# Four fused attention layers on one core: layer 3's mask tables tied to their row of layer 2, and the values of layer 3's first two rows made in layer 2's last row

## The chip, the core and the metric

The kernel runs on one core of a Trainium2 chip. The metric is device time in microseconds of one execution. A core has five engines that run their own instruction streams in order and meet through semaphores: PE (TensorE, matrix products), DVE (VectorE), ACT (ScalarE), POOL (GpSimd) and SP (SyncE, which here only issues transfers between memory and the core's SBUF). PE writes its products to PSUM, from which DVE and ACT read them.

## The reference

Four images of 56 x 56 pixels with 256 channels go through four layers, each of the form x = x + f(group norm of x). Layer 2 is neighbourhood attention (a 7 x 7 window around every pixel, half of the heads dilated by 2), layer 3 is attention in shifted 7 x 7 windows with a position bias and a mask. What the change touches, cut from the reference:

```python
# layer 3, on the group norm of layer 2's result
xs = jnp.roll(x, (-3, -3), axis=(1, 2))              # then cut in windows of 7 x 7
qkv = xw @ qkv_weight.T + qkv_bias
q, k, v = (qkv[0] * hd ** (-0.5), qkv[1], qkv[2])
attn = jnp.einsum('whnd,whmd->whnm', q, k) + bias    # bias = rel_bias_table[rel_index]
attn = attn.reshape(B, nW, HEADS, N, N) + mask[None, :, None]
attn = jax.nn.softmax(attn, axis=-1)
out = jnp.einsum('whnm,whmd->wnhd', attn, v)
out = out @ proj_weight.T + proj_bias                # rolled back, and x = x + out
...
x = x + _L2_conv_ref(_gn(x), ...)
x = x + _L3_conv_ref(_gn(x), ...)
```

## The kernel before, in words

`direct_blocks` runs the layers one after the other, with all activations in float32 and the images handed from layer to layer through DRAM.

**Layer 2** (`layer2`) goes through 16 rows (4 images, 4 strips of 14 image rows). In this text row r is one of the 16, and unit r.u is one of its 8 units of attention, u = 0 to 7. `attend_pairs` takes the units in turn. For unit u it issues the logits (PE, L1067, into `ps_s`, of which there is one pair); DVE adds a bias to one half of them (L1074) and ACT takes the exponential (L1075); of the other half ACT takes the exponential first (L1077) and POOL multiplies it (L1078). Then POOL adds up pairs of the unit before (`both`, L1087), the unit's extra work is issued (`fill`), and PE makes the products of the unit before (L1096). After them come DVE's reciprocal (L1960), ACT's look at it (L998) and DVE's scaling into `attn` (L1964, L1970). The gathers of a unit's values from DRAM (`vp<-vd`, L1954, SP) go to one of three buffers, so a gather can be issued when the products of the third unit before are done.

The extra work of a row is laid out in `work[0]` to `work[7]`: projecting the input of a row ahead (`project_rows`: values L979, keys and queries L952), normalising one more (`prepare`, ACT, L942), and the output projection of the row before (`project_out`, L952 and then DVE L1995 and L896, in four steps at u = 2, 3, 6, 7). Rows 14 and 15 have nothing left to project: row 14 has `project_rows` work in its first half only, row 15 only output projections. After the last row come the tail (`both` and `products` of unit 15.7) and the output projection of row 15.

In rows 1 to 4, `work[7]` also takes a step of `table_steps`: layer 3's mask tables. Each of four steps adds a table to the looked up bias on DVE (L2058, two instructions), takes an exponential of part of it on ACT (L2060) and stores it to `m3d` in DRAM (L2062). The order of layer 2 on each engine comes from a scheduler that works with its own estimates of time and puts an instruction where it finds it ready. It put all four steps right at the start of layer 2, and likewise layer 3's load of the first half of the tables (`m3a`, L2097).

**Layer 3** (`layer3`) goes through 32 rows of 7 image rows, in an order that is written out by hand for PE, DVE, ACT and POOL. Before its first attention it has a head: `prepare(0)` and `prepare(1)` normalise two rows on DVE (L945, six instructions each), `values` of rows 0 and 1 (PE L979, DVE L983, stored to DRAM L987, read back in another layout by `gather`, L2147), the keys and queries of row 0 (`project_rows(0)`), and `prepare(2)`.

SBUF is handed out in pools that are closed in the reverse order of opening. Layer 2's input pool (`brief`: `xn2`, `v2`, `q2`) stands on the left side and stays open until layer 2 ends; layer 3's pools stand on the right.

Of the kernel before, what the change touches and what calls it, by code (L numbers as in the profile page):

```python
# [830 lines left out]
def direct_blocks(ctx: ExitStack, tc: tile.TileContext, d: dict, watch):  # L831
# [136 lines left out]

    def value_tiles(v, a, c, n, xn, w, bias, dst):

        t0, t1 = c * n // P, (c + 1) * n // P if (c + 1) * n < T else -(-T // P)
        pm = ps_m()
        sizes = [min(P, T - t * P) for t in range(t0, t1)]
        mine = sizes[2 * a:2 * a + 2]
        for j, k in enumerate(mine):
            first = (2 * a + j) * P
            for h in range(CC):
                for i in range(0, k, HD):
                    nc.tensor.matmul(pm[i:i + HD, j * C:(j + 1) * C], lhsT=xn[:, h, first + i:first + i + HD], rhs=w[:, h, :],  # L979
                                     start=(h == 0), stop=(h == CC - 1))  # L980
        for k in sorted(set(mine)):
            js = [j for j, kj in enumerate(mine) if kj == k]
            nc.vector.tensor_tensor(  # L983
                v[:k, 2 * a + js[0]:2 * a + js[-1] + 1, :], pm[:k, js[0] * C:(js[-1] + 1) * C].rearrange("p (j c) -> p j c", c=C),
                bias[:k].rearrange("p (o c) -> p o c", o=1).to_broadcast([k, len(js), C]), ALU.add)
            t = t0 + 2 * a + js[0]
            nc.sync.dma_start(out=dst[t * P:min((t + len(js)) * P, T), :].rearrange("(k p) c -> p k c", p=k),  # L987
                              in_=v[:k, 2 * a + js[0]:2 * a + js[-1] + 1, :])
# [64 lines left out]

    def attend_pairs(pool, units):

# [47 lines left out]
        for w in units:  # L1103
# [7 lines left out]
            held = w  # L1111
        both(held)
        products(held)
        held["done"]()
# [736 lines left out]

    def layer2(held, big, pool, brief, last_steps, ends):

        nonlocal m_bufs
        m_bufs = 2
        xs, load, w_qkv, bias = (held[n] for n in ("xs", "load", "w", "bias"))
        xns, q, attns, ahead = {}, {}, {}, []
# [127 lines left out]
        def project_out(r):  # L1985
# [13 lines left out]
            return [lambda m=m, y=y: step(y, m) for y in range(2) for m in range(CC)]  # L1999

        def stream():
            n = NIMG * NSB
            for r in range(n):
                attns[r] = pool.tile([P, CC, 2 * WC2], FP, tag="attn", name="attn2")
                work = [[] for _ in range(8)]
                for y, i in enumerate((2 * r + 3, 2 * r + 4)):
                    if i < 2 * n:
                        v0, v1, k0, k1, q0, q1 = lazily(project_rows, i, 6)
                        for a, steps in enumerate(((v0, k0), (v1, q0), (k1,), (q1,))):
                            work[4 * y + a] += steps  # L2010
                    if i + 1 < 2 * n:
                        work[4 * y + 3].append(lambda i=i: prepare(i + 1))
                if r:
                    for u, step in zip((2, 3, 6, 7), project_out(r - 1)):
                        work[u].append(step)
                for u in (1, 4, 5):
                    work[u].insert(0, step_stats)
                if r and table:
                    work[7].append(table.pop(0))
                for u, w in enumerate(pair(r, m, i) for i in range(4) for m in range(2)):  # L2020
                    w["fill"] = lambda steps=work[u]: [f() for f in steps]
                    yield w
# [15 lines left out]
        table.append(tables.close)  # L2038
        attend_pairs(pool, stream())
        for step in project_out(NIMG * NSB - 1):  # L2040
# [5 lines left out]
    def table_steps(big, pool):  # L2046
# [7 lines left out]
        def mask(ty):  # L2054
            m = pool.tile([98, NH, 98], FP, tag="m3", name="m3")
            for w in range(2):
                sl = slice(w * WN, (w + 1) * WN)
                nc.vector.tensor_tensor(m[:, :, sl], found.rearrange("p q h -> p h q"), t3[:, ty:ty + 1, sl].to_broadcast([98, NH, WN]), ALU.add)  # L2058
            mv = m.rearrange("p (q j) k -> p q j k", j=4)[:, :, 2:4]
            nc.scalar.activation(mv, mv, AF.Exp)  # L2060
            for pair in [3] if ty % 2 else range(3):
                nc.sync.dma_start(out=m3d[:, ty // 2, :, pair, :], in_=m)  # L2062
# [13 lines left out]

    def layer3(early, big, pool, brief):
        def image_rows(wr):
# [8 lines left out]

        xs, xns, vs, qk, attns, ahead = {}, {}, {}, {}, {}, []
        vd = [dram.tile([T, C], FP, name=f"vd3_{b}") for b in range(NIMG)]
# [4 lines left out]

        load(0)
        m3 = [big.tile([98, NH, 4 * 98], FP, name="m3a")]
        nc.sync.dma_start(out=m3[0], in_=m3d[:, 0].rearrange("p h w k -> p h (w k)"))  # L2097
        w_qkv = weight(early, "wqkv3", 3 * C)
        w_p = weight(pool, "wp3", C)
        m3.append(pool.tile([98, NH, 4 * 98], FP, name="m3b", bufs=1))  # L2100
        nc.sync.dma_start(out=m3[1], in_=m3d[:, 1].rearrange("p h w k -> p h (w k)"))

# [7 lines left out]

        def prepare(r):
            x = xs.pop(r)
            if r + 1 < NIMG * 8:
                load(r + 1)
            c = r % 8
            xn = xns[r] = early.tile([P, CC, 448], FP, tag="xn", name="xn3", bufs=3)
            at = left(c, WC)
            for h in range(CC):
                for w, xv in parts(xn[:, h, at:at + WC], x[:, h, :]):
                    normalise(w, xv, known(3, r // 8), h)  # L2120
            if at:
                end = left(c - 1, WC) + WC
                nc.scalar.copy(xn[:, :, :at], ahead[0][:, :, end - at:end])
            ahead[:] = [xn]

        def project_rows(r):
# [22 lines left out]
        def values(r):  # L2149
# [5 lines left out]
            def step(a):  # L2155
                value_tiles(v, a, c, WC, xn, w_qkv[:, :, 2 * C:], bv3, vd[b])
                if a == 0 and r:
                    gather(r - 1)
# [4 lines left out]
        def quad(r, hq, single=False):  # L2163
# [22 lines left out]

            mk = m3[wr // 7][:, 4 * hq:4 * hq + 4, :]
            i = 2 * (NIMG * 8 + r) + hq
# [56 lines left out]

        prepare(0)
        prepare(1)
        for r in range(2):
            for step in values(r):
                step()  # L2250
        for step in project_rows(0):
# [26 lines left out]

    ends, firsts, passing, begun = ExitStack(), ExitStack(), ExitStack(), []

    def begin_layer1():
# [5 lines left out]
        begun[:] = [[few] + first, late]  # L2287
        return steps

    def run(l, layer, fixed, kinds):  # L2290
# [16 lines left out]
    with pool_of(2, 0) as early:  # L2307
        held = {}
        last_steps = run(1, lambda own: layer1(*own, first, late, lambda: layer2_ahead(early, held)), {E.PE, E.DVE}, range(3))
        firsts.close()  # L2310
        run(2, lambda own: layer2(held, *own, last_steps, ends), None, range(1, 4))
    run(3, lambda own: layer3(own[1], own[0], *own[2:]), {E.PE, E.DVE, E.Activation, E.Pool}, (1, 0, 2, 3))
    return newest[0].ins
# [101 lines left out]
```

## Time and profile before

| what | us |
|---|---|
| median of 3 runs | 3770.52 (3767.21 to 3772.34) |
| the profiled execution | 3769.93 |
| its span | 3768.0 |
| PE busy | 3665.8 (97%) |
| DVE busy | 2200.9 (58%) |
| ACT busy | 1472.2 (39%) |
| POOL busy | 1815.9 (48%) |

Layer 2 begins in the span at about 2600 us and layer 3's head at about 3250 us. Two stretches around these points, and one of layer 2's steady part between them:

| stretch, us | PE busy | DVE | ACT | POOL | granted PE clock |
|---|---|---|---|---|---|
| 2628 to 2670 (42.0) | 35.21 | 24.40 | 24.28 | 25.19 | 0.96 |
| 2670 to 2710 (40.0) | 39.95 | 28.41 | 27.89 | 32.61 | 1.00 |
| 3215.4 to 3245.4 (30.0), row 15 | 26.55 | 24.73 | 15.91 | 29.17 | 0.94 |
| 3245.4 to 3257.6 (12.2), tail and output projection | 10.58 | 9.33 | 2.08 | 3.58 | 0.72 |

A row of this kind gives the busy time of each engine in the stretch, and the share of its full clock that PE was granted. A timeline row gives start and length of an instruction, or of several of one kind that follow each other (x4), the engine ("SPq" is SP issuing a transfer, "PEld" PE loading weights), the line, what is written from what, and in brackets the idle time before it with what ended it. The profile counts a float32 matmul as two passes.

### The profile page before, as it was taken

Reading aid. Unit: us, or ns where it says so; the run is one execution under the profiler, and the core shown is the slowest. Engines: PE = TensorE matmul, PEld = TensorE weight load, DVE = VectorE, ACT = ScalarE, POOL = GpSimd, SP = SyncE. Lnnn points to the kernel's source line nnn. Section 1 sums busy time; section 2 is a strip of 40 time slices with the busy share of each in tenths; the row PEclk is TensorE's granted clock in tenths of the full one; section 3 lists DMA queues with packets and bytes.
Section 4 is the critical chain, followed back from the end, with each engine's and each line's share of the span. In section 5 each row is a group of like instructions: output and inputs, shape, how many; then the busy total and the mean of one; then the engine's idle time right before and its main releaser. Section 6 shows DMA issues by size and latency. Waiting matters only on the chain. (4 is left out here: it accounts for less than half of the span.)

```text
span 3768.0 us, 112324 instructions
## 1 busy us (share of the span) xinstructions
PE 3665.8 (97%) x48826; PEld 2478.1 (66%) x48826; DVE 2200.9 (58%) x4188; ACT 1472.2 (39%) x3125; POOL 1815.9 (48%) x1966
## 2 busy tenths in 40 slices
PE   8999999999999999999999999999999999999998
PEld 4555556677776777767777667775666666555554
DVE  5777777634445444464344544445676777777676
ACT  5565566422222222222222222222666666444443
POOL 4777777612235222352222421123777777555555
PEclk9999999999999999999999999999999999999999
DMA  6544444300010000011000000002544444534443
GB/s 213 169 153 134 132 123 137 134 7 23 23 27 29 22 19 18 21 32 28 19 16 22 26 20 10 11 20 78 138 133 137 132 128 119 155 126 139 130 134 99
DMA packets 278039, 304.94 MB, mean 81 GB/s; under 512 B 33624, under 2 KB 268764, under 8 KB 277084
## 3 DMA queue, kind: packets, MB, share of 16 engines
q1 hardware_dynamic: 275680, 297.43, 25.7%
q8 instruction: 385, 6.31, 0.7%
q0 software_dynamic: 1568, 0.16, 0.1%
q14 instruction: 118, 0.97, 0.1%
q10 hardware_dynamic: 288, 0.08, 0.0%
HBM read 205.04 MB, written 92.55 MB: 79 GB/s over the span
## 5 line engine op out<-in xcount | busy, mean ns | idle before, releaser
L1564 DVE TENSOR_TENSOR acc<-acc,ps_v 128x257 f32<-128x257 f32 x1104 | 463.8, 422 | 781.8 <-PE ps_v L1642 753.4
L1642 PE MATMUL ps_v<-xw,e 128*128 128x257 f32 x2208 | 611.0, 381 | 3.4 <-DVE xnT L1509 2.2
L1637 PE MATMUL ps_o<-xw,at 128*128 128x257 f32 x2208 | 609.0, 379 | 0.0
L1532 PE MATMUL ps_s<-xnT,xd 128*128 128x512 f32 (+3 forms) x1344 | 571.4, 548 | 3.9 <-DVE xnT L1509 3.9
L1626 ACT COPY at<-ps_t 128x512 f32<-128x512 f32 (+3 forms) x332 | 170.6, 514 | 960.9 <-PE ps_t L1623 960.7
L1642 PEld LDWEIGHTS ps_v<-xw,e 128*128 128x128 f32 x2208 | 413.4, 189 | 144.6 <-issue 83.2
L1087 POOL TENSOR_TENSOR b<-e 126x336 f32<-126x336 f32 (+5 forms) x512 | 499.5, 997 | 7.7
L1637 PEld LDWEIGHTS ps_o<-xw,at 128*128 128x128 f32 x2208 | 419.1, 190 | 60.1
L952 PE MATMUL ps_m<-xn,w_wqkv 128*32 128x392 f32 x4096 | 376.4, 496 | 8.0 <-ACT gst L917 3.4
L1525 POOL TENSOR_SCALAR xd<-xnT,vec 128x128 f32<-128x128 f32 x192 | 116.4, 616 | 478.0 <-PE ps_s L1532 477.8
L1078 POOL TENSOR_TENSOR e<-e,m0t 126x672 f32<-126x672 f32 (+3 forms) x128 | 238.8, 1865 | 182.1 <-ACT e L1077 180.6
L1535 ACT ACTIVATE e<-ps_s 128x512 f32<-128x512 f32 x336 | 185.4, 552 | 355.0 <-PE ps_s L1532 351.8
L1532 PEld LDWEIGHTS ps_s<-xnT,xd 128*128 128x128 f32 x1344 | 225.4, 191 | 141.4 <-issue 126.2
L1078 POOL TENSOR_TENSOR e<-e,bias 119x784 f32<-119x784 f32 (+5 forms) x128 | 239.4, 1870 | 157.3 <-ACT e L1077 156.9
L1096 PEld LDWEIGHTS ps_o<-e,vp 124*32 124x32 f32 (+3 forms) x8192 | 200.3, 110 | 101.9 <-issue 84.1
L998 ACT ACTIVATE no<-rs 128x168 f32<-128x168 f32 (+2 forms) x256 | 94.0, 367 | 426.0 <-DVE rs L1960 190.2
L952 PEld LDWEIGHTS ps_m<-xn,w_wqkv 128*32 128x32 f32 x4096 | 123.8, 110 | 183.1 <-issue 128.6
L1960 DVE RECIPROCAL rs<-ps_o 128x196 f32<-128x196 f32 (+2 forms) x128 | 175.7, 1372 | 109.7 <-PE ps_o L1096 108.0
L1096 PE MATMUL ps_o<-e,vp 124*32 124x112 f32 (+3 forms) x8192 | 232.2, 249 | 3.1 <-POOL e L1078 2.5
L1075 ACT ACTIVATE e<-e 126x672 f32<-126x672 f32 (+5 forms) x256 | 219.7, 858 | 13.3 <-DVE e L1074 1.9
L1077 ACT ACTIVATE e<-ps_s 126x672 f32<-126x672 f32 (+5 forms) x256 | 206.3, 806 | 5.4 <-PE ps_s L1067 3.0
L979 PE MATMUL ps_m<-w_wqkv,xn 128*32 128x256 f32 x3136 | 196.9, 381 | 2.1 <-DVE v L983 1.6
(214 smaller groups left out, 5945.5 us busy)
## 6 DMA issues: line engine op xcount, KB each, us to landing
x<-xr SPq DMA_DIRECT2D x64, 392.0 KB
x<-in_x SPq DMA_DIRECT2D x53, 448.0 KB
x<-x SPq DMA_DIRECT2D x60, 392.0 KB
xr<-x SPq DMA_DIRECT2D x60, 392.0 KB
vd<-v SPq DMA_DIRECT2D x72, 256.0 KB
xr<-in_x SPq DMA_DIRECT2D x32, 392.0 KB
xr<-x SPq DMA_DIRECT2D x28, 448.0 KB
x<-xr SPq DMA_DIRECT2D x28, 448.0 KB
```

What stands on the lines that cost most here:

```text
L952: nc.tensor.matmul(pm[j * HD:(j + 1) * HD, :n], lhsT=w[:, h, col + j * HD:col + (j + 1) * HD], rhs=rhs(h), start=(h == 0), stop=(h == CC - 1))
L979: nc.tensor.matmul(pm[i:i + HD, j * C:(j + 1) * C], lhsT=xn[:, h, first + i:first + i + HD], rhs=w[:, h, :], start=(h == 0), stop=(h == CC ...
L1075: nc.scalar.activation(ev, ev, AF.Exp)
L1077: nc.scalar.activation(ev, sv, AF.Exp)
L1078: nc.gpsimd.tensor_tensor(parts(ev), parts(ev), w["emask"], ALU.mult)
L1087: nc.gpsimd.tensor_tensor(w["b"][a][:nk, :, :2 * nq].rearrange("p h (i c) -> p h i c", i=2), ev[:, :, :, 0, :], ev[:, :, :, 1, :], ALU.add)
L1096: nc.tensor.matmul(w["o"](k, i)[j * HD:(j + 1) * HD], lhsT=ones[:nk, :HD] if k else v(j, u), rhs=w["b"][j // 2][:nk, j % 2, i * nq:(i + 1) ...
L1532: nc.tensor.matmul(s[:, :n], lhsT=xd[j][:, h, :], rhs=xnT[:, h, first * P:last * P], start=(h == 0), stop=(h == CC - 1))
L1535: nc.scalar.activation(e[:, :n], s[:, :n], AF.Exp, scale=5.0)
L1564: nc.vector.tensor_tensor(acc[:, i, :], acc[:, i, :], pv[:, :C + 1], ALU.add)
L1637: nc.tensor.matmul(out[j][:, :C + 1], lhsT=e[:, col(i)] if i == j else at[:, col(i)], rhs=xw[:, i, :], start=(i == j), stop=(i == NB - 1))
L1642: nc.tensor.matmul(pv[:, :C + 1], lhsT=e[:, col(i)], rhs=xw[:, j, :], start=True, stop=True)
```

## The change

1. The two additions of a mask step get an edge behind the newest bias addition of layer 2 on DVE (`tc.issue_after(newest[0].ins)`), so that each step stands in its own row, 1 to 4.
2. Layer 2 opens its input pool itself (`passing`) and closes it in unit 14.4, when the last input is projected. The queries of rows 14 and 15 move to a small pool on the right (`d2q`). The first part of layer 3 (`layer3_ahead`) opens its pools there, over the closed pool's memory.
3. In units 14.4 to 14.7 the first steps of layer 3 are issued: the loads of its first rows, its qkv weights in three parts, `prepare(0)` and `prepare(1)`, now on ACT, and the load of half of the first mask table (`m3a` is split in `m3a` and `m3c`, four heads each).
4. The values of layer 3's rows 0 and 1 are made in six steps of one or two tiles: at u = 0, 1, 4, 5 of row 15 and two in the tail, between `both` and `products`. Layer 3's head keeps `gather(0)`, `project_rows(0)` and `prepare(2)`.
5. In row 14 the four steps of the output projection stand at u = 4, 5, 6, 7 instead of 2, 3, 6, 7.

```diff
-    def value_tiles(v, a, c, n, xn, w, bias, dst):
+    def value_tiles(v, a, c, n, xn, w, bias, dst, some=range(2), pm=None):
-        pm = ps_m()
+        pm = ps_m() if pm is None else pm
...
         for j, k in enumerate(mine):
+            if j not in some:
+                continue
...
+        if len(mine) - 1 not in some:
+            return pm
...
-    def attend_pairs(pool, units):
+    def attend_pairs(pool, units, tail=()):
...
         both(held)
+        for step in tail:
+            step()
         products(held)
...
-    def layer2(held, big, pool, brief, last_steps, ends):
+    def layer2(held, big, pool, last_steps, ends, begin_layer3):
+        passing, values3 = ExitStack(), []
+        brief = passing.enter_context(pool_of(2, 3))
...
+        def begin():
+            passing.close()
+            steps3[:], values = begin_layer3(1)
+            values3.extend(values)
+            steps3[0]()
...
+                if r == n - 4:
+                    q[n - 2], q[n - 1] = begin_layer3(0)
...
-                    for u, step in zip((2, 3, 6, 7), project_out(r - 1)):
+                    for u, step in zip((4, 5, 6, 7) if r == n - 2 else (2, 3, 6, 7), project_out(r - 1)):
                         work[u].append(step)
+                if r == n - 2:
+                    work[4].append(begin)
+                    for u in range(1, 4):
+                        work[4 + u].append(lambda u=u: steps3[u]())
+                if r == n - 1:
+                    for u in (0, 1, 4, 5):
+                        work[u].append(lambda: values3.pop(0)())
...
-        attend_pairs(pool, stream())
+        attend_pairs(pool, stream(), [lambda: values3.pop(0)()] * 2)
...
-                nc.vector.tensor_tensor(m[:, :, sl], found.rearrange("p q h -> p h q"), t3[:, ty:ty + 1, sl].to_broadcast([98, NH, WN]), ALU.add)
+                with tc.issue_after(newest[0].ins):
+                    nc.vector.tensor_tensor(m[:, :, sl], found.rearrange("p q h -> p h q"), t3[:, ty:ty + 1, sl].to_broadcast([98, NH, WN]), ALU.add)
...
-        m3 = [big.tile([98, NH, 4 * 98], FP, name="m3a")]
-        nc.sync.dma_start(out=m3[0], in_=m3d[:, 0].rearrange("p h w k -> p h (w k)"))
-        w_qkv = weight(early, "wqkv3", 3 * C)
+        m3 = big.tile([98, 4, 4 * 98], FP, name="m3a")
+        w_qkv = early.tile([P, CC, 3 * C], FP, name="w_wqkv3", bufs=1)
+        def load_weight(k):
...
-        def prepare(r):
+        def prepare(r, normal=normalise):
...
-                    normalise(w, xv, known(3, r // 8), h)
+                    normal(w, xv, known(3, r // 8), h)
...
+        def values(r):
+            v, pms = own.tile([P, 4, C], FP, tag="vt", name="vt3", bufs=1), []
+            def step(a, some, *pm):
+                pms.append(value_tiles(v, a, r, WC, xns[r], w_qkv[:, :, 2 * C:], bv3, vd[0], some, *pm))
+            return [lambda: step(0, (0,)), lambda: step(0, (1,), pms[0]), lambda: step(1, (0,))]
+
+        steps = [lambda: (load(0), load_weight(2)), lambda: (prepare(0, normalise_act), load_weight(1)),
+                 lambda: (prepare(1, normalise_act), load_weight(0)),
+                 lambda: nc.sync.dma_start(out=m3, in_=m3d[:, 0, :4].rearrange("p h w k -> p h (w k)"))]
+        return [transfer, xns, vd, m3, w_qkv, parts, prepare], steps, lazily(values, 0, 3) + lazily(values, 1, 3)
+
+    def layer3(front, pool):
+        m3 = [[m3, pool.tile([98, 4, 4 * 98], FP, name="m3c", bufs=1)]]
+        nc.sync.dma_start(out=m3[0][1], in_=m3d[:, 0, 4:].rearrange("p h w k -> p h (w k)"))
...
-        prepare(0)
-        prepare(1)
-        for r in range(2):
-            for step in values(r):
-                step()
+        gather(0)
         for step in project_rows(0):
             step()
         prepare(2)
...
+    def begin_layer3(part):
+        open_pool = lambda name, bufs: fronts.enter_context(
+            tc.tile_pool(name=name, bufs=bufs, side="right", reuse_waits="tile"))
+        if part == 0:
+            few = open_pool("d2q", 1)
+            return [few.tile([P, CC, 2 * WC2], FP, name=f"q2_{i}") for i in range(2)]
+        front3[:], steps, values = layer3_ahead(open_pool("d3", 1), open_pool("d3e", 2), open_pool("d3v", 1))
+        return steps, values
```

More of the change, by code (lines that the diff above doesn't have):

```diff
@@ L1999, in project_out @@
             return [lambda m=m, y=y: step(y, m) for y in range(2) for m in range(CC)]
+        def begin():
[3 more added lines that the diff above has]
+            steps3[0]()
+        steps3 = []
         def stream():
@@ L2075, in check_sizes, with layer3_ahead @@
         nc.vector.tensor_reduce(watch[1][:, 2 * CC + 1:], pos[:, :CC], AX.X, ALU.add)
-    def layer3(early, big, pool, brief):
+    def layer3_ahead(big, early, own):
         def image_rows(wr):
@@ L2086, in transfer @@
                 nc.sync.dma_start(out=ends[out], in_=ends[1 - out])
-        xs, xns, vs, qk, attns, ahead = {}, {}, {}, {}, {}, []
+        xs, xns, ahead = {}, {}, []
         vd = [dram.tile([T, C], FP, name=f"vd3_{b}") for b in range(NIMG)]
@@ L2093, in load @@
             transfer(3, r, xs[r], 0)
-        load(0)
-        m3 = [big.tile([98, NH, 4 * 98], FP, name="m3a")]
-        nc.sync.dma_start(out=m3[0], in_=m3d[:, 0].rearrange("p h w k -> p h (w k)"))
-        w_qkv = weight(early, "wqkv3", 3 * C)
-        w_p = weight(pool, "wp3", C)
-        m3.append(pool.tile([98, NH, 4 * 98], FP, name="m3b", bufs=1))
-        nc.sync.dma_start(out=m3[1], in_=m3d[:, 1].rearrange("p h w k -> p h (w k)"))
+        m3 = big.tile([98, 4, 4 * 98], FP, name="m3a")
+        w_qkv = early.tile([P, CC, 3 * C], FP, name="w_wqkv3", bufs=1)
+        def load_weight(k):
+            nc.sync.dma_start(out=w_qkv[:, :, k * C:(k + 1) * C],
+                              in_=d["wqkv3"].rearrange("(h p) o -> p h o", p=P)[:, :, k * C:(k + 1) * C])
         def parts(win, x):
@@ L2124, in prepare @@
             ahead[:] = [xn]
+        def values(r):
[8 more added lines that the diff above has]
+    def layer3(front, pool):
+        transfer, xns, vd, m3, w_qkv, parts, prepare = front
+        vs, qk, attns = {}, {}, {}
+        m3 = [[m3, pool.tile([98, 4, 4 * 98], FP, name="m3c", bufs=1)]]
+        nc.sync.dma_start(out=m3[0][1], in_=m3d[:, 0, 4:].rearrange("p h w k -> p h (w k)"))
+        w_p = weight(pool, "wp3", C)
+        m3b = pool.tile([98, NH, 4 * 98], FP, name="m3b", bufs=1)
+        m3.append([m3b[:, :4], m3b[:, 4:]])
+        nc.sync.dma_start(out=m3b, in_=m3d[:, 1].rearrange("p h w k -> p h (w k)"))
         def project_rows(r):
@@ L2156, in step @@
                 value_tiles(v, a, c, WC, xn, w_qkv[:, :, 2 * C:], bv3, vd[b])
-                if a == 0 and r:
+                if a == 0:
                     gather(r - 1)
@@ L2185, in piece @@
                         lambda j: vs[r][:, u, (4 * hq + j) * HD:(4 * hq + j + 1) * HD], True, True)
-            mk = m3[wr // 7][:, 4 * hq:4 * hq + 4, :]
+            mk = m3[wr // 7][hq]
             i = 2 * (NIMG * 8 + r) + hq
@@ L2279, in direct_blocks @@
     ends, firsts, passing, begun = ExitStack(), ExitStack(), ExitStack(), []
+    fronts, front3 = ExitStack(), []
     def begin_layer1():
@@ L2310, in direct_blocks @@
         firsts.close()
-        run(2, lambda own: layer2(held, *own, last_steps, ends), None, range(1, 4))
-    run(3, lambda own: layer3(own[1], own[0], *own[2:]), {E.PE, E.DVE, E.Activation, E.Pool}, (1, 0, 2, 3))
+        run(2, lambda own: layer2(held, *own, last_steps, ends, begin_layer3), None, range(1, 3))
+    run(3, lambda own: layer3(front3, *own), {E.PE, E.DVE, E.Activation, E.Pool}, (2,))
+    fronts.close()
     return newest[0].ins
```

## The prediction

> **What bounds the kernel now.** The page gives PE busy for 97% of the span, so what can be won lies where PE stands still or is throttled. I read the slices of the page first (PE is full but for the joints of the layers), then busy times by stretch around layer 2's two ends:
>
> ```profile
> 3191.00:3203.60 12.60, 12.04 (x308) 7.95 (x304) 10.18 (x15) 6.62 (x17) 8.16 (x8) 1.00 0.31 98
> 3203.60:3249.20 45.60, 38.97 (x1012) 26.84 (x1012) 37.16 (x51) 23.55 (x47) 44.12 (x36) 0.95 0.44 134
> 3249.20:3263.60 14.40, 14.03 (x173) 8.28 (x174) 10.16 (x24) 0.66 (x3) 0.00 (x0) 0.79 0.49 159
> ```
>
> Columns: length, busy PE, weight loads, DVE, ACT, POOL, granted clock, DMA share, GB/s. From unit 14.4 on (second row) POOL is busy 44.12 of 45.6 us: rows 14 and 15 run at POOL's pace, and PE idles 6.6 us. Before it PE sets the pace and POOL idles 12.6 - 8.16 = 4.4 us. After it comes layer 3's head, PE alone at a clock of 0.79.
>
> The timeline at layer 2's beginning:
>
> ```profile
> 2627.32 2.84 PE L952 MATMUL ps_m<-xn,w_wqkv 128*32 128x392 f32 x32
> 2630.09 3.15 DVE L2058 TENSOR_TENSOR m<-found,t 98x392 f32<-98x392 f32 x4 [2.23 <-DMA found<-looked_up]
> 2631.74 0.53 ACT L2060 ACTIVATE m<-m 98x392 f32<-98x392 f32 x1 [4.98 <-DVE m L2058]
> 2632.18 0.35 ACT L1896 ACTIVATE kE<-ps_m,vec 128x133 f32<-128x133 f32 x1
> 2633.36 4.53 PE L952 MATMUL ps_m<-xn,w_wqkv 128*32 128x392 f32 x32 [2.84 <-ACT kE L1896]
> ...
> 2650.42 0.53 PE L1096 MATMUL ps_o<-b,ones 85*32 85x98 f32 x12 [0.97 <-POOL b L1087]
> 2652.44 0.94 PE L1067 MATMUL ps_s<-q,k2t 32*85 32x98 f32 x32 [1.49 <-DVE e L1074]
> ```
>
> The mask waits for a transfer, ACT stands behind the mask though the keys it has to copy are ready, and PE waits 2.84 us for ACT. After it 32 passes take 4.53 us instead of 2.84.
>
> And at its end:
>
> ```profile
> 3202.62 0.90 ACT L1077 ACTIVATE e<-ps_s 124x896 f32<-124x896 f32 x1
> 3203.60 2.10 POOL L1078 TENSOR_TENSOR e<-e,bias 124x896 f32<-124x896 f32 x1 [1.15 <-ACT e L1077]
> ...
> 3249.90 8.04 PE L952 MATMUL ps_m<-attn,w_wp 128*32 128x392 f32 x62
> 3257.61 2.92 PE L979 MATMUL ps_m<-w_wqkv,xn 128*32 128x256 f32 x48
> 3260.86 2.80 PE L979 MATMUL ps_m<-w_wqkv,xn 128*32 128x256 f32 x48 [0.32 <-DVE vt L983]
> ```
>
> **1. Masks in their rows: -7.0 us.** Built, the changed kernel has each pair of L2058 behind an L1074 of its row and no mask in the first units. Gone: PE's 2.84; 1.49 and 0.97, which come of DVE standing 1.77 us for a mask's store (`m3d<-m`) and POOL's L1087 taking 3.28 and 2.72 us instead of 2.24 and 1.75; and the half clock behind the gap, 4.53 - 2.84 = 1.7. Sum 7.0. PE's other waits there (values at 2610, group statistics) stay. What is next late is PE itself, busy 39.95 of 40 us from 2670 on. Bounds: -4.5 (the first gap and its clock alone) to -8.
>
> In rows 1 to 4 a step costs DVE 1.8 to 3.2 us once a row (0.9 to 1.6 each at L2058) and ACT 0.53. There DVE is busy 28.41 of 40 us and PE comes back for the logits buffer 2.3 us after DVE has freed it (L1074 ends at 3183.45, L1067 at 3185.74), with 1 to 3 us of DVE idle ahead of it. I take 0; at worst 1 us in each of two rows, +2. SP's stores move too (eight, 0.35 to 0.5 us each) into a queue that has some 8 us spare per row; 0. The load of `m3a` (1.2 MB) leaves 2666, where PE waited for no transfer; 0.
>
> [...]
>
> **2. Values out of the head: -5.7 us.** The two groups of 48 passes, 3257.61 to 3263.59, are 5.98 us. Each of the six steps is 16 passes, 0.97 us. Four go to row 15 where PE idles: 3.9 of 6.6 us, hidden by POOL. Without that cover they would cost their 3.9. Two go to the tail, 1.9 us against PE waits of 0.60 + 0.66 + 0.36 = 1.6: +0.3. DVE's four L983 (2.2 us) lie in DVE's idle 8 us of the second row above.
>
> **3. Output projection moved within row 14.** Units 14.2 and 14.3 lose 16 passes each, 1.33 us, and 14.4 and 14.5 get them under POOL. Followed through (logits 14.3 at 3194.6, products 14.2 done at 3198.2, POOL's L1087 of 14.3 done at 3201.2) POOL could begin 14.4 at 3201.2 instead of 3203.60: -2.4, if ACT is in time.
>
> **4. ACT is not in time: the new wait.** In the changed order four of the normalisations of `prepare(0)` stand on ACT ahead of the exponential of 14.4, and most of `prepare(1)` ahead of that of 14.5. They wait for loads which SP issues only behind the gathers of 14.4 and 14.5. Before, the gather of 14.4 is issued from 3195.72 to 3200.56; products 14.1 are 1.3 us earlier now, so it ends at 3199.1. A load takes 3.4 us (`found`, issued 2626.72, used 2630.09) to 3.95 (first input load, 0.73 to 4.68). So x(0) is there at about 3202.7, while ACT would be free at 3199.9. Behind it:
> - four activations, 0.58 + 0.2 + 0.2 + 0.58 = 1.6 us (L942 x 392 has 0.63 start to start, small ones like L1877 0.2): exponential 14.4 at 3204.3, POOL at 3205.4 instead of 3203.60: +1.8;
> - x(1), behind the gather of 14.5, issued 3203.3, there at about 3207; five activations, L998, two more: exponential 14.5 at 3209.6, POOL at 3210.5 instead of 3207.85: +2.65;
> - the scheduler also puts `prepare(2)` on DVE (six L945, about 1.7 us) into units 14.5 to 14.7, behind x(2) (there at about 3212.2), ahead of the bias and reciprocal of 14.5 to 14.7; together with the moved projection (L1995 and L896, 1.1 us a step) DVE frees exponential 14.7 at 3218.6, POOL at 3219.5 instead of 3215.22: +4.3.
>
> Queued behind ACT's wait are the exponentials, behind them POOL, PE's products and, since `ps_s` is single, PE's next logits (idle some 3.6 us). From there POOL is the limit to the end, so +4.3 stands. Ends: -2.4 (loads early, no wait) to +8 (each of three loads 1.3 us later). SP has three weight parts, half a mask, loads and stores more, 5 us over 12 units, where it waited about 5; I take 0.
>
> **5. Clock at the joint: -1.5 us.** Between 3250 and 3255 PE was granted 0.50, and the 62 passes took 8.04 us. [...] The trace throttles it after gaps of 0.66 us at most. [...] After the last `attn` (3252.0) some 3 us ran at half: -1.5. The new gap's half clock falls into POOL's and ACT's time: 0. Ends: -2.5 to 0.
>
> **Sum**: -7.0 - 5.7 + 4.3 - 1.5 = -9.9. Layer 3 behind the head is PE bound (35.78 of 36.4 us), so it moves as a whole. `gather(0)` now stands behind 2 MB of tables and weights, 2 MB at the 0.26 to 0.3 MB/us of that stretch, (1.2 + 0.6 + 0.26), and lands near 3271, first products near 3276: 0, at worst +2. Against the profiled execution, 3769.93 - 9.9 = 3760.0; the median lies 0.6 above it: **3760.6**.
>
> **Rivals.**
> - *No wait on ACT* (loads there before the exponentials): part 4 becomes -2.4, sum -16.6, 3753.9. For it: POOL's room is there. Against: the order of SP and ACT, and 3.4 us per load.
> - *The end gives nothing*: parts 2 to 5 cancel because the three waits add up to +7.2 instead of 4.3, and of part 1 only the first gap is won: -4.5, 3766. For it: DVE, ACT and POOL are all close to full in row 14. Against: a shift there is bounded by 1.3 us per load.
> - *Slower*: the same held ACT, but with the gathers of 14.6 and 14.7 late too, as they queue on SP and in the rings behind 2.4 MB of loads (three inputs of 0.39 MB, weights 0.77, half a mask 0.6 by the page's sizes, less what has landed by then). At 0.28 MB/us (262 to 303 GB/s between 3260 and 3270) that is 8.6 us; PE's products wait, POOL's e buffers (two) fill. It decides from a POOL delay of 14.2 us (7.0 + 5.7 + 1.5); at 4.3 + 8.6 + 10 for a second such round: 3779. Against: a gather is needed only a unit and a half after its issue.
> - That the masks are not moved is excluded by the built order.
>
> **Numbers.** Forecast 0.56, own range 3756 to 3764; no wait 0.22; end gives nothing 0.17; slower 0.05. Range 3753 to 3767 leaves out the slow case and the edges of the others. What a measurement can tell from no change is 0.2%, 7.5 us, so faster means below 3763.0: 0.88 of the forecast, all of the second, a fifth of the third: 0.74. Slower 0.05, same 0.21.
>
> **What will show it.** No mask in the first units and no half clock near 2634; logits 0 some 4.9 us earlier against layer 2's first keys. Around 14.4 ACT idle 2 to 3 us in front of L942 with a transfer as releaser, and POOL idle about 4 us there. Two L979 groups gone from the head, `project_rows(0)` 9 to 10 us earlier in the span. If POOL is full from 14.4 on, part 4 is wrong; if row 15 takes more than 31 us, part 2 is.

## The result and the profile after

| kernel | median of the runs, us | range | profiled execution (span) |
|---|---|---|---|
| before | 3770.69 (22 runs) | 3766.01 to 3777.99 | 3769.93 (3768.0) |
| after | 3764.60 (22 runs) | 3760.85 to 3769.81 | 3761.59 (3759.8) |

The ratio of after to before is 0.9985, 95% interval 0.9979 to 0.9992: 5.7 us less, with 3.0 to 7.9 in the interval. The forecast was 3760.6, so 4 us of the expected 9.9 did not come. The median lies 0.6 above the range that the forecast itself was given (3756 to 3764) and inside the range that was stated for the whole (3753 to 3767). A time below 3763.0 was held likely (0.74); the median is not below it.

A gain of this size can't be read from one span: code that the change doesn't touch shifts it by as much (last section). So the two executions are compared place by place: when does the logits group of unit r.u start (L1067 before, L1071 after), after minus before, and how much does that difference grow over a stage? Minus is time won.

| stage | after minus before, us | predicted |
|---|---|---|
| layers 0 and 1 (code unchanged) | -4.0 | 0 |
| layer 2's opening, to the end of row 0 | -8.6 | -7.0 |
| rows 1 to 5, with the masks in them | +5.0 | 0 |
| rows 6 to 13 | 0.0 | 0 |
| rows 14 and 15 | +6.9 | +4.3 |
| joint: from the last logits to `project_rows(0)` | -7.6 | -7.2 (steps 2 and 5) |
| the change alone (the five stages without layers 0 and 1) | -4.4 | -9.9 |

Behind the joint layer 3 moves as a whole: at the end of the span after is 0.2 us later than this sum says.

Busy times of after by stretch, with the columns of the prediction (length; busy PE, weight loads, DVE, ACT, POOL; granted clock; DMA share; GB/s):

```profile
3183.00:3196.00 13.00, 11.39 (x310) 7.83 (x302) 10.68 (x14) 5.81 (x15) 8.43 (x8) 1.00 0.42 121
3196.00:3214.30 18.30, 12.69 (x284) 8.37 (x284) 11.24 (x19) 11.40 (x27) 11.28 (x9) 0.81 0.76 217
3214.30:3248.30 34.00, 30.84 (x836) 21.42 (x836) 29.33 (x42) 17.50 (x35) 32.98 (x27) 1.00 0.43 128
3248.30:3255.00 6.70, 5.91 (x76) 2.43 (x80) 4.86 (x8) 0.46 (x2) 0.01 (x1) 1.00 0.26 91
```

The second row is units 14.4 to 14.7, and no engine is full in it: POOL, full from 14.4 on before, does 11.28 of 18.3 us, PE 12.69 at a clock of 0.81. The third row is POOL's again. The fourth ends where `project_rows(0)` begins, at full clock.

The opening, in after's timeline (start, length, engine, line, what is written from what):

```profile
2620.29 2.77 PE L981 MATMUL ps_m<-w_wqkv,xn 128*32 128x256 f32 x48
2623.01 5.63 PE L952 MATMUL ps_m<-xn,w_wqkv 128*32 128x392 f32 x64
2628.57 0.62 PE L1071 MATMUL ps_s<-q,kE 32*95 32x112 f32 x10
```

PE goes from the values through all keys and queries to the last logits of unit 0.0 without a gap: the wait of 2.84 us and the group at half clock are gone, as predicted (granted clock 1.00 from 2610 to 2645).

In the rows, a mask step in after's timeline (row 1):

```profile
2699.42 3.22 DVE L2084 TENSOR_TENSOR m<-found,t 98x392 f32<-98x392 f32 x2
...
2699.56 2.42 POOL L1082 TENSOR_TENSOR e<-e,bias 119x784 f32<-119x784 f32 x1 [1.31 <-ACT e L1081]
...
2701.95 2.22 POOL L1091 TENSOR_TENSOR b<-e 119x392 f32<-119x392 f32 x2
...
2703.23 0.33 SPq L2088 DMA_DIRECT2D m3d<-m  x1
2703.66 0.45 SPq L2006 DMA_DIRECT2D x<-xr  x1
...
2704.16 2.56 SPq L2088 DMA_DIRECT2D m3d<-m  x2
...
2706.87 0.81 SPq L991 DMA_DIRECT2D vd<-v  x1
...
2707.78 8.16 SPq L1962 DMA_DIRECT2D vp<-vd  x8
```

Two things cost here. DVE's pair takes 3.2 us, and beside it POOL's L1082 and L1091 take 2.4 and 2.2 us instead of 1.9 and 1.7. And three stores stand on SP ahead of the gathers of `vp`: from 2701.6, when the gathers before them are issued, to 2707.8 SP issues no gather. PE doesn't stop in this row, since gathers run ahead of their use; it stops two rows on, when they no longer do (the same timeline, products of unit 3.2, which took 0.77 us in before; with the wait 1.55 us are lost here):

```profile
2760.06 1.62 PE L1100 MATMUL ps_o<-e,vp 126*32 126x84 f32 x32 [0.51 <-DMA vp<-vd]
```

And row 14, in after's timeline (SP's two lines are the loads of layer 3's first and third input):

```profile
3191.59 0.47 SPq L2113 DMA_DIRECT2D x<-x  x1
...
3196.00 1.87 ACT L942 ACTIVATE xn<-x,gst 128x343 f32<-128x343 f32 x4 [3.65 <-DMA x<-x]
3198.70 1.92 PE L1071 MATMUL ps_s<-q,k2t 32*119 32x98 f32 x28 [4.31 <-ACT e L1081]
3198.73 2.08 POOL L1082 TENSOR_TENSOR e<-e,bias 124x896 f32<-124x896 f32 x1 [5.31 <-ACT e L1081]
...
3200.55 2.75 PE L952 MATMUL ps_m<-attn,w_wp 128*32 128x392 f32 x16
...
3201.08 0.41 SPq L2113 DMA_DIRECT2D x<-x  x1
...
3203.38 0.63 DVE L2003 SCALAR_TENSOR_TENSOR xr<-ps_m,vec,xr 128x392 f32<-128x392 f32 x1 [2.04 <-PE ps_m L952]
...
3203.67 1.87 POOL L1082 TENSOR_TENSOR e<-e,bias 119x784 f32<-119x784 f32 x1 [0.65 <-ACT e L1081]
...
3206.74 0.69 DVE L945 TENSOR_SCALAR xn<-x,gst 128x343 f32<-128x343 f32 x1 [0.58 <-DMA x<-x]
...
3208.47 1.81 DVE L945 TENSOR_SCALAR xn<-x,gst 128x28 f32<-128x28 f32 x3
...
3214.32 1.86 POOL L1082 TENSOR_TENSOR e<-e,bias 119x784 f32<-119x784 f32 x1 [3.33 <-ACT e L1081]
```

ACT stands at the first input's load as forecast (3.65 us, where 2.8 had been reckoned, then four activations), PE and POOL behind it. POOL's units 14.5 and 14.7 in before (14.4 is shown in the prediction, 3203.60):

```profile
3207.85 1.85 POOL L1078 TENSOR_TENSOR e<-e,bias 119x784 f32<-119x784 f32 x1
...
3215.22 1.85 POOL L1078 TENSOR_TENSOR e<-e,bias 119x784 f32<-119x784 f32 x1 [0.27 <-ACT e L1077]
```

Against these places, moved by the 7.69 us won until then, POOL begins units 14.4, 14.5 and 14.7 late by 2.8, 3.5 and 6.8 us; forecast were 1.8, 2.65 and 4.3. PE's products wait for no gather there, so the rival "slower" does not show.

### The profile page after: what moved, and what is told of

Same layout as the page of the kernel before. It is cut to its first block, busy times and chain, and to the rows that moved or that the text cites. A ratio compares the mean times of both kernels' runs of the same rounds, so it can differ in the third digit from the quotient of the medians.

```text
span 3759.8 us, 112322 instructions
## 1 busy us (share of the span) xinstructions
PE 3658.0 (97%) x48826; PEld 2473.3 (66%) x48826; DVE 2203.2 (59%) x4176; ACT 1476.2 (39%) x3137; POOL 1818.2 (48%) x1966
## 4 chain that ended last, share of the span: by engine, by line
PE 86%; DVE 7%; ACT 2%; POOL 2%; issue 2%; DMA 1%; SPq 0%; DVEq 0%; ACTq 0%; POOLq 0%
PE ps_m L952 17%; PE ps_o L1643 14%; PE ps_s L1538 13%; PE ps_v L1648 13%; PE ps_m L981 6%; PE ps_o L1100 5%; PE ps_s L1071 5%; PE ps_t L1629 3%; PE ps_o L1040 2%; PE ps_s L1024 2%; PE ps_m L1503 1%; DVE e L1078 1%; DVE rs L1255 1%; POOL b L1091 1%; PE ps_v L1609 1%
## 5 line engine op out<-in xcount | busy, mean ns | idle before, releaser
L1091 POOL TENSOR_TENSOR b<-e 126x336 f32<-126x336 f32 (+5 forms) x512 | 499.6, 997 | 7.7
L1082 POOL TENSOR_TENSOR e<-e,m0t 126x672 f32<-126x672 f32 (+3 forms) x128 | 238.8, 1865 | 178.4 <-ACT e L1081 176.7
L1082 POOL TENSOR_TENSOR e<-e,bias 119x784 f32<-119x784 f32 (+5 forms) x128 | 241.5, 1887 | 158.4 <-ACT e L1081 157.8
L1081 ACT ACTIVATE e<-ps_s 126x672 f32<-126x672 f32 (+5 forms) x256 | 206.3, 806 | 5.5 <-PE ps_s L1071 5.5
```

The lines of the kernel that those rows point to most:

```text
L1081: nc.scalar.activation(ev, sv, AF.Exp)
L1082: nc.gpsimd.tensor_tensor(parts(ev), parts(ev), w["emask"], ALU.mult)
L1091: nc.gpsimd.tensor_tensor(w["b"][a][:nk, :, :2 * nq].rearrange("p h (i c) -> p h i c", i=2), ev[:, :, :, 0, :], ev[:, :, :, 1, :], ALU.add)
```

## Experiments

Each kernel was profiled once and timed in five rounds beside the kernel before. The stages are those of the table above; "net" is the sum up to `project_rows(0)`, without layers 0 and 1, against the one profile of before. The kernel before had another median beside each group of experiments: 3770.95 us beside e1, e3, e4 and e5, 3768.07 beside e2, e6, e7 and e8, 3770.12 beside e9 to e12. So kernels of different groups are compared by the ratio, not by the median.

| kernel | opening | rows 1-5 | rows 14, 15 | joint | net | median, us | ratio to before (95%) |
|---|---|---|---|---|---|---|---|
| after | -8.6 | +5.0 | +6.9 | -7.6 | -4.4 | 3764.60 | 0.9985 (0.9979 to 0.9992) |
| e12, the same again | -6.9 | +4.1 | +7.2 | -7.6 | -3.3 | 3764.93 | 0.9986 (0.9978 to 0.9995) |
| e1, no mask tie | +1.3 | 0.0 | +6.6 | -7.6 | +0.2 | 3773.14 | 1.0006 (0.9998 to 1.0014) |
| e2, mask tie alone | -8.7 | +3.0 | 0.0 | -1.8 | -7.4 | 3764.21 | 0.9989 (0.9983 to 0.9996) |
| e4, stores on ACT | -8.1 | +15.6 | +7.9 | -7.6 | +7.7 | 3777.25 | 1.0016 (1.0008 to 1.0024) |
| e6, stores spread | -8.6 | +0.8 | +9.1 | -7.7 | -5.8 | 3763.56 | 0.9984 (0.9978 to 0.9991) |
| e7, additions spread too | -8.7 | 0.0 | +8.1 | -7.6 | -8.2 | 3761.60 | 0.9980 (0.9973 to 0.9987) |
| e3, ACT tied | -6.7 | +3.6 | +8.1 | -7.6 | -2.7 | 3767.13 | 0.9989 (0.9980 to 0.9997) |
| e5, ACT and DVE tied | -8.5 | +4.1 | +1.6 | -4.2 | -7.0 | 3763.14 | 0.9976 (0.9966 to 0.9985) |
| e8, third input in row 15 | -6.8 | +2.0 | +6.0 | -7.6 | -6.5 | 3760.38 | 0.9975 (0.9966 to 0.9984) |
| e9, its load in row 15 too | -8.6 | +3.2 | +5.4 | -7.2 | -7.1 | 3761.53 | 0.9982 (0.9973 to 0.9990) |
| e11, e9 without the shift | -6.7 | +3.5 | +9.6 | -6.3 | 0.0 | 3764.76 | 0.9985 (0.9978 to 0.9991) |
| e10, e7 and e9 together | -8.9 | 0.0 | +6.1 | -7.3 | -9.9 | 3760.61 | 0.9976 (0.9966 to 0.9987) |

A rest of up to 0.6 us lies in rows 6 to 13 (e6 0.6, e10 0.2).

### The two halves apart: e1 and e2

e1 takes the edge out of the changed kernel; e2 puts it alone into the kernel before:

```diff
-                with tc.issue_after(newest[0].ins):
-                    nc.vector.tensor_tensor(m[:, :, sl], found..., ALU.add)
+                nc.vector.tensor_tensor(m[:, :, sl], found..., ALU.add)
```

> The changed kernel, with the tie of the eight mask additions taken out again, so that the masks stand in layer 2's opening as before. Theory of the two traces (the tie wins 8.6 us at the start of layer 2 and gives 5.0 back in rows 1 to 5): 3.6 us slower than the changed kernel, about 3768.2, with the stores gone from the rows and no gather late there. Rival, as predicted (rows 1 to 4 cost nothing, so what was lost there is something else): 7 to 8.6 us slower, 3772 to 3773, and the loss in rows 2 to 5 is there without masks too.

> The kernel before, with the tie of the mask additions alone and nothing else of the change. By the two traces and the run without the tie (8.6 us won at the start of layer 2, 5.0 given back in rows 2 to 5): 3.5 to 5 us faster than before, about 3766.5, and no gain or loss in rows 14 and 15. By the prediction's step 1 (rows 1 to 4 cost nothing): 7 us faster, 3764.

Without the tie the kernel is no faster than before: the values made early and all that goes with them are worth nothing in sum (+6.6 in rows 14 and 15, and at the joint what e2 lacks, 5.9). The tie alone makes 4.1 us by the ratio.

e1's time is that of its rival, but the place decides against the rival: without masks in them rows 1 to 5 lose nothing, so what is lost there is the masks'. Its median is 4.9 us above the 3768.2 of its theory. Its opening is part of this, 1.3 us worse than that of the kernel before: PE stands behind masks that wait for a store (timeline of e1):

```profile
2641.47 1.62 DVE L2083 TENSOR_TENSOR m<-found,t 98x392 f32<-98x392 f32 x2 [5.60 <-DMA m3d<-m]
...
2644.03 1.96 PE L1071 MATMUL ps_s<-q,kI 32*90 32x84 f32 x32 [3.26 <-DVE e L1078]
```

Most of the rest no trace explains: by the medians e1 is 8.5 us slower than after, by the two profiles 4.6, and e1's profiled execution (3766.23) is the fastest of its 13. The other 3.9 us stay open.

Over the eight profiles with the masks placed as in the change (after, e12, e2, e3, e5, e8, e9, e11) the rows lose 2.0 to 5.0 us, 3.5 in the mean.

### What the masks cost in their rows: e4, e6, e7

e4 issues the stores from ACT. e6 issues one store per half row and a mask only in every second row; e7 also puts the two additions of a mask half a row apart.

```diff
# e4
-                nc.sync.dma_start(out=m3d[:, ty // 2, :, pair, :], in_=m)
+                nc.scalar.dma_start(out=m3d[:, ty // 2, :, pair, :], in_=m)
# e6, e7
-                if r and table:
-                    work[7].append(table.pop(0))
+                for u in (3, 7):
+                    if r and table:
+                        work[u].append(table.pop(0))
...
# e6: A(ty) adds both halves, S(ty, pair) is one store
+        return [no_step, A(0), S(0, 0), S(0, 1), S(0, 2), A(1), S(1, 3), no_step, ...]
# e7: A(ty, w) adds one half
+        return [A(0, 0), A(0, 1), S(0, 0), S(0, 1), S(0, 2), A(1, 0), A(1, 1), S(1, 3), ...]
```

> The changed kernel, with the eight stores of the masks issued by ACT's queue instead of SP's; the additions stay in their rows. Theory S (the stores stand in SP's queue ahead of the gathers of vp and make these late; PE waits for vp at 3.4, 4.2 and 4.3): those waits go and 3 to 4 us of the 5.0 lost in rows 1 to 5 come back, about 3761. Rival C (the additions on DVE and POOL's work hold each other up, L1082 at 2.4 instead of 1.9 us and L1091 at 2.2 instead of 1.7): the loss stays, 3764 to 3765, and ACT's issuing can only add to it.

> The changed kernel, with the masks' eight stores spread, one to a half row instead of up to three in a row, and a mask only in every second row; the pairs of additions stay whole. Theory S (stores in a row on SP make the gathers of vp late): the losses of the unit 3.4 and of 4.2 and 4.3 (about 3 us of 5.0) go, those right behind an addition's unit (3.0, 5.1, 5.2; about 1.5 us) stay: about 3761.5. Rival C (additions): rows lose 5 us as before, only later, 3764.6.

> As e6_stores_spread, and the two additions of a mask half a row apart. If the pair of additions in one unit (3.2 us of DVE, POOL's L1082 and L1091 0.5 us longer each beside it) is what costs the rest: another 1 to 1.5 us, rows lose under 1 us in all, about 3760. If single additions cost as much each: as e6_stores_spread.

e4 does not decide between its theories by its time, since it moves the wait instead of taking it away. Its timeline:

```profile
2706.68 7.42 ACTq L2088 DMA_DIRECT2D m3d<-m  x3
2714.15 0.34 ACT L1002 ACTIVATE no<-rs 128x168 f32<-128x168 f32 x1 [6.89 <-DMA m3d<-m]
...
2716.28 1.92 PE L1071 MATMUL ps_s<-q,k2t 32*119 32x98 f32 x28 [5.87 <-ACT e L1081]
```

ACT's issuing of three stores lasts 7.42 us, with the exponentials behind it: 8.6 us are lost in row 2 and 5.5 in row 4, each behind a mask of which three stores go out at once. But row 3, which lost 1.55 us at unit 3.4 in after, loses nothing at that unit.

e6 agrees with theory S in its trace: 1.4 us are left of the 3.5 (the least of the eight profiles is 2.0), lost at units 2.6, 4.2 and 8.2, behind the masks of rows 1, 3 and 7. Its ratio, 0.9984 against after's 0.9985, doesn't tell this from no change. In e7's profile, and again in e10's, nothing is left. All its masks, as one tile's list of instructions (durations in ns: least, median, most; nothing waited for them):

```profile
L2089 DVE TENSOR_TENSOR m<-found,t x8: 881/896/901, 2685.3 to 2955.8; 98x392 f32<-98x392 f32 x8
L2095 SPq DMA_DIRECT2D m3d<-m x8: 422/432/499, 2706.7 to 2958.0; - x8
```

The same list in after:

```profile
L2084 DVE TENSOR_TENSOR m<-found,t x8: 880/1648/2411, 2699.4 to 2819.1; 98x392 f32<-98x392 f32 x8
L2088 SPq DMA_DIRECT2D m3d<-m x8: 330/612/1688, 2703.2 to 2823.3; - x8
```

The median of 1648 is no duration of anything: in each pair of after the first addition takes 0.9 and the second 2.4 us. The first is issued 0.14 us ahead of POOL's L1082, which then takes 0.55 us more (2.42 instead of 1.87); the second ends 0.66 us behind L1082's end. In e7 the one addition came first in all eight places: DVE pays 0.9 there, and no unit is late. So the pairs of additions had a share of the loss. That the stores had the other share fits e4's unit 3.4 but is not shown by e6, which also sets its masks two rows apart.

### Row 14: e3, e5, e8, e9

e3 ties the ACT normalisations of the first two inputs behind the newest exponential (L1081); e5 also ties the third input's, on DVE, behind row 15's last L1078; e8 traces them in unit 15.2 instead; e9 moves the third load to 15.0 and them to 15.5.

```diff
# e3, in prepare(r)
+            with tc.issue_after(newest_act[0].ins) if r < 2 else nullcontext():
+                prepare_now(r, normal)
# e5, in layer3
+        with tc.issue_after(newest[0].ins):
+            prepare(2)
# e8, in row 15; e9: load(2) in work[0], third in work[5]
+                    work[2].append(third)
```

> The changed kernel, with the ACT normalisations of layer 3's first two inputs tied behind the newest exponential of L1081, so that no exponential of row 14 stands behind a wait for a load. Theory A (ACT's wait for x(0) and x(1) is what makes row 14 lose 6.8 us): the waits of 3.65 us of L942 and of 4.3 us of PE at 14.4 and 14.5 go, and 4 to 6 us come back, about 3759 to 3761. Rival B (row 14 is limited by DVE and POOL anyhow: DVE's normalisations of the third input and the moved output projection take the place of the wait): under 2 us come back, 3763 or more.

> As e3_act_tied, and the six DVE normalisations of the third input tied behind row 15's last L1078, out of units 14.5 to 14.7. Theory A with the step that followed it (DVE frees the bias late at 14.7): 1 to 2 us more than e3_act_tied, about 3758. Rival: DVE has room there once ACT is in time, and both kernels take the same time; or the six stand in the joint's way and cost up to 1.7 us.

> As e3_act_tied, and the third input's normalisations traced in row 15 and tied on DVE behind the L1078 of unit 15.2, where DVE waits for POOL; in e3_act_tied DVE waited 8.3 us for that input's load ahead of a bias addition, in e5_act_dve_tied the six stood ahead of the last xr of the tail (PE waits 3.4 us). Theory A (an engine that takes its work in order waits behind a normalisation for its load, on ACT in the changed kernel, on DVE in e3): neither wait is left, rows 14 and 15 lose under 2 us of the 6.8, the joint keeps its 7.6: 5 us faster than the changed kernel, about 3760. Rival: POOL sets the end of layer 2 anyhow, and moving them changes under 1.5 us.

> As e8_act_dve15, with the load of the third input moved to unit 15.0 and its normalisations to 15.5. In e8 the load stands on SP in the middle of the gather of unit 14.5's vp, waits there until its buffer is free, and PE waits 2.18 and 1.29 us for vp. Theory A' (the wait for a load or its buffer only went on from ACT to DVE to SP, each an engine that works in order): rows 14 and 15 lose under 1.5 us instead of 6 to 8, which is 4 to 6 us better than the changed kernel: about 3758 to 3760. Rival: POOL's pace alone sets rows 14 and 15: they lose 5 us or more again.

In e3 ACT waits for no load any more and unit 14.7 starts 2.5 us earlier than in before's pace. Then DVE does what ACT had done (timeline of e3):

```profile
3212.84 0.48 DVE L945 TENSOR_SCALAR xn<-x,gst 128x343 f32<-128x343 f32 x1 [8.30 <-DMA x<-x]
...
3216.41 1.85 POOL L1082 TENSOR_TENSOR e<-e,bias 119x784 f32<-119x784 f32 x1 [8.91 <-ACT e L1081]
```

DVE stands 8.3 us in front of the third input's load, with a bias addition behind it, and rows 14 and 15 lose 8.1 us as a whole. With that gone in e8, SP is next (timeline of e8):

```profile
3207.79 0.68 PE L1100 MATMUL ps_o<-e,vp 126*32 126x84 f32 x16 [2.18 <-DMA vp<-vd]
3207.87 0.37 SPq L2118 DMA_DIRECT2D x<-x  x1
3208.30 1.55 SPq L1962 DMA_DIRECT2D vp<-vd  x2
...
3209.77 0.97 PE L1100 MATMUL ps_o<-e,vp 126*32 126x84 f32 x16 [1.29 <-DMA vp<-vd]
```

The third load stands between two halves of a gather (that of unit 14.6, not 14.5 as the expectation of e9 has it), and PE waits for both. In e9 that load is later, and the six normalisations stand together in one unit (timeline of e9):

```profile
3231.00 5.27 DVE L945 TENSOR_SCALAR xn<-x,gst 128x343 f32<-128x343 f32 x6
...
3239.00 1.62 POOL L1082 TENSOR_TENSOR e<-e,bias 90x672 f32<-90x672 f32 x1 [3.35 <-ACT e L1081]
...
3239.03 0.93 PE L1071 MATMUL ps_s<-q,k2t 32*85 32x98 f32 x32 [2.80 <-DVE e L1078]
```

They take 5.27 us beside POOL, where 1.7 had been reckoned. In e5 they stand in the tail, and PE waits for the `xr` behind them (timeline of e5):

```profile
3247.98 1.10 PE L981 MATMUL ps_m<-w_wqkv,xn 128*32 128x256 f32 x16 [3.38 <-DVE xr L2003]
```

Rows 14 and 15 lose only 1.6 there, but the joint gives 4.2 instead of 7.6. So theory A holds for each wait by itself and was wrong about the sum: in each of these profiles some 5 us or more of the 7 are lost in another queue. By the ratio e3 is no better than after, and e5, e8 and e9 are 1 to 4 us better, with intervals that overlap after's. POOL's pace alone does not set these rows (POOL waits up to 8.9 us in them).

### The moved projection, and both repairs: e11, e10, e12

e11 is e9 with the output projection at units 2, 3, 6, 7 of row 14 again; e10 joins e7's masks to e9; e12 is the changed kernel once more, beside these.

```diff
# e11
-                    for u, step in zip((4, 5, 6, 7) if r == n - 2 else (2, 3, 6, 7), project_out(r - 1)):
+                    for u, step in zip((2, 3, 6, 7), project_out(r - 1)):
```

> As e9_load_late, without the shift of row 13's output projection within row 14 (units 2, 3, 6, 7 again). By the prediction's step 3 the shift is worth 2.4 us once ACT is in time: 2.4 us slower than e9_load_late. Rival: PE is not late at 14.4 once POOL is the limit, and both take the same time within 0.5 us in rows 14 and 15.

> The stores and additions spread as in e7_all_spread together with e9_load_late. If the two losses are separate they add: rows 2 to 13 lose nothing, rows 14 and 15 under 1.5 us; about 3 to 4 us better than e9_load_late and 8 to 10 better than the changed kernel, 3755 to 3757. If they are not separate (SP is the common limit of both and its queue in row 14 is no better): as e9_load_late.

> The changed kernel itself, beside the three others on the same chip, as the measure for what they gain: 3764 to 3766; rows 14 and 15 lose 6 to 8 us and rows 1 to 5 lose 2 to 5 us as in its first profile.

With the shift unit 14.4 starts 2.5 us earlier in each of the profiles that has it; without it, not at all. In e11 rows 14 and 15 lose 4.2 us more than in e9 and the median is 3.2 higher; the intervals of the two ratios overlap, and e11's profiled execution (3769.91) is the slowest of its 21, with half clock for 6.8 us at 3222 and again at 3246 (0.90 in the mean from 3196 to 3250). So the start of 14.4 is shown, and what the shift is worth at the end is not. e10 loses nothing in rows 1 to 5, but 6.1 us in rows 14 and 15, where under 1.5 had been expected. It has the best net of all, -9.9, which happens to be the forecast for the change; its median is 4.3 us below e12's, from 8 executions, and its interval still overlaps those of e12 and after. A version that is better than after beyond doubt was not found, only several (e5, e7, e8, e10) whose ratios lie 2 to 4 us below.

## Where the prediction held and where not

- **Step 1, opening.** Right in its mechanism: PE's wait, the half clock behind it and the late store are gone. It gave 6.7 to 8.7 us over the eight profiles, against 7.0. The lower values belong to the four executions (e12, e3, e8, e11) in which PE's clock was halved for 3.4 us from 2613 to 2615 on, in unit 0.0.
- **Step 1, rows 1 to 4: the first term that was mis-sized.** Forecast 0, at worst 2; measured 2.0 to 5.0, mean 3.5. The prediction counted eight stores against SP's spare 8 us a row and found room. Spare time in a row is no measure for a queue whose gathers are needed at set times: three stores, the first waiting for its mask, kept the gathers off SP for 6 us. For DVE it reckoned 1.8 to 3.2 us a step; every step took the upper end, 3.2, as 0.9 and 2.4. In after's pairs the cost went by the order: 0.55 us to POOL's L1082 beside the addition that came before it (2.42 instead of 1.87), 1.5 us to the addition that came behind L1082's start (2.4 instead of 0.9). Stores and additions spread together cost nothing (0.0 in e7 and e10); how the 3.5 us divide between them stays open.
- **Step 2, values out of the head.** Right. From the last group of the output projection to `project_rows(0)` e2, without the early values, takes 10.1 us, after 4.3: 5.8 less, forecast 5.7. From logits 15.0 to 15.7 after loses 0.3 us, with the four steps of row 15 in between, which were reckoned as hidden.

e2's joint in its timeline:

```profile
3244.52 4.46 PE L952 MATMUL ps_m<-attn,w_wp 128*32 128x392 f32 x48 [0.63 <-DVE attn L1964]
3248.80 2.77 PE L979 MATMUL ps_m<-w_wqkv,xn 128*32 128x256 f32 x48
3251.87 2.80 PE L979 MATMUL ps_m<-w_wqkv,xn 128*32 128x256 f32 x48 [0.30 <-DVE vt L983]
3254.61 5.47 PE L952 MATMUL ps_m<-xn,w_wqkv 128*32 128x392 f32 x64
```

And after's:

```profile
3250.85 4.46 PE L952 MATMUL ps_m<-attn,w_wp 128*32 128x392 f32 x48 [0.63 <-DVE attn L1972]
3255.12 5.45 PE L952 MATMUL ps_m<-xn,w_wqkv 128*32 128x392 f32 x64
```

- **Step 5, clock at the joint.** In the profiles it gave its size (1.8 against 1.5), but not for its reason. That the thin tail had halved the clock, and that values in it would keep the clock up, was the author's estimate, and no run shows this term: e2 has no values in the tail, waits there up to 0.66 us as the kernel before does, and runs the same 48 passes as after in the same 4.46 us. The half clock of before (0.50 from 3249 to 3255; after was granted 1.00 from 3248.3 to 3255.1) stands in its one profile and not in e2's, where row 15 and the joint have the same code, so it was no sure term in a sum for medians.
- **Step 3, projection moved.** Right: logits 14.4 start 2.5 us earlier in every profile that has it, forecast -2.4 for POOL. Where ACT is in time (e3) POOL too begins 14.4 2.5 us earlier; in after ACT's wait takes it back, as forecast.
- **Step 4, ACT's wait: the second term that was mis-sized.** The mechanism was right in each part (ACT at the loads, POOL behind it, then DVE's six L945), its size was +6.9 and +7.2 instead of +4.3. Three terms were short. The first and third load took 4.4 and 5.7 us from issue to use, not 3.4 to 3.95; why is not shown (the traffic was 194 and 251 GB/s while they were under way, and 214 and 208 for the two loads from which the price came). The new gap's half clock (granted 0.50 to 0.55 from 3196 to 3203.3) was priced at 0, but 16 passes of the moved projection ran in it (2.75 us instead of 1.5) and DVE waited 2.04 us for them. And the six L945 took 3.1 us beside POOL instead of 1.7, between the bias additions of 14.5 and 14.7. How the 2.7 us that are missing divide among the three was not tested.

With the measured terms the sum is -7.7 (mean of the eight openings) + 3.5 - 5.8 + 7.0 = -3.0, at the near end of the measured 3.0 to 7.9; how often the half clock of before's joint (1.8 us) falls in other executions is not known. The two terms that were mis-sized cost 6.2 us more than forecast; that the median came no further from the forecast than 4 us is in part luck: 2.7 us lie between this sum and the measured 5.7, and no trace accounts for them. The chances of the prediction also do not add up as it says: 0.56 x 0.88 + 0.22 + 0.17 / 3 is 0.77 for "faster", not 0.74.

Of the rivals, "no wait on ACT" is out, by ACT's 3.65 us, and "the end gives nothing" (3766) came nearer than the forecast: its waits add up to 7.2, as it said, and what the opening wins less what the rows lose, 4.2, is near its 4.5, though for another reason. It had been given 0.17 because a shift was thought bounded by 1.3 us per load.

## What to carry to other kernels

When a step is moved under other work, look at each queue that it joins for the next instruction behind it that is needed at a set time, not for spare time per row. Here a wait for a load stood ahead of such an instruction on ACT (after), then on DVE (e3), then on SP (e8), and each time it was taken off one queue, 5 us or more of the 7 were lost in another. Split a step so that each queue gets one short piece at a time; in the profiles of e7 and e10 the masks became free by that. And test the halves of a change by themselves: here, within the intervals, one half made the whole gain, and the other gave back in row 14 what it won behind it.

## What the runs showed of the hardware

- The granted clock dipped where nothing in the code has changed. The end of layer 0 lies 4.5 us earlier to 1.3 us later than in the profile of before in the profiles of after and the twelve experiments, all with the same code up to there. This is as much as the change's whole gain. The largest step lies where the clock is halved in one profile and not in the other: before has half clock (0.50) for 6.8 us at 483.5 and after none there (1.00 from 475 to 490), and 2.6 us of the difference arise at that place.
- Two DVE additions in a row, the first 0.14 us ahead of POOL's L1082, take 0.88 to 0.90 and 2.39 to 2.43 us in all 40 pairs of the ten profiles with the tie and whole pairs; one alone takes 0.88 to 0.90 in all eight places of e7. In before, where POOL's instruction had begun 1.2 us ahead of a pair, both took longer, 1.58 and 1.69 us.
- DVE's normalisation L945 of 28 elements takes 0.28 us alone and 1.77 us in e9, where POOL's L1082 starts 0.19 us ahead of it (1.91 us) and both end together; in e5, e10 and e11 it is 1.76 to 1.78 us in the same place. So in these places L945 lasted about as long as what was left of POOL's instruction, 1.72 us in e9.
- Three stores issued by ACT held ACT for 7.42 us at the first mask of e4, while SP was issuing gathers; in after SP took 2.0 to 2.6 us for two in a row. So moving the stores to the other issuing engine did not make them free here; why the third came 6.1 us after the second is not shown.
